# One layer of attention and routed experts on one core: gate/up and down products of a step set half a step apart

## The chip, the core and the metric

The kernel runs on one core of a Trainium2 chip. The metric is device time in microseconds (us), from launch to end. In the rows of the profile PE is TensorE, PEld its weight loads, DVE VectorE, ACT ScalarE, POOL GpSimd, and SPq the queue of SyncE, which issues most DMAs. Each engine takes its instructions in a fixed order that was written when the program was built; an instruction that waits for a semaphore holds up everything behind it on its engine.

## What is computed

Input x has 2048 tokens of 512 values, all in float32. The layer normalizes each token (xn), and adds three things to x:

```
rvk = xn @ W_rvk.T ; r, v, k = split(rvk)          # three products of 512 x 512 per token
y   = sigmoid(r) * wkv(time_decay, time_first, k, v)  # a recurrence along the tokens
attention = y @ W_out.T
logits = xn @ classifier.T ; two of 12 experts per token by softmax + bias
expert e < 8:  down_e( silu(gate_e(xn)) * up_e(xn) ),  inner width 256
expert e >= 8: xn itself                               # no weights
out = x + attention + sum of the two experts, each with its weight
```

## The kernel before

**Blocks and units.** The tokens are cut into four blocks of 512 (`b`) and each block into four rows of 128 tokens (`j`; row `i = 4b + j`, so 16 rows). The 512 channels are cut into four chunks (`c`). A unit is one (b, c): `project` (L259) makes k, v and r of it by three groups of four products, each 128x128 by 128x512, added up in a PSUM bank of the pool `ps_mm` (two banks). After the fourth product of a group ScalarE copies the bank to SBUF (L278 for k and v, L276 for r, an exponential); a new group waits for the copy of the group two before it. `scan` (L282) then runs the recurrence of the unit in four stages: VectorE prepares (L293 to L300); ScalarE takes two exponentials (L302, L303); VectorE makes the sums (L309 to L318); last come small copies of the state (POOL L321, ScalarE L322) and on VectorE a reciprocal (L323) and a product (L324). After the four chunks of a block, `attention` (L719) multiplies the block by W_out: four products for each row of 128 tokens, then VectorE adds the result to the row (L740), and an accumulating DMA on POOL's queue adds it to the output in DRAM (L743).

**Experts.** Routing is worked out early. Tokens are sorted by expert into 25 tiles of 128 places, and a tile goes through this chain, `i` being the tile:

- `gather` (POOL, L556): an indirect DMA fetches its 128 tokens.
- `flip` (ScalarE copy `xp`, L594; then a transposing DMA on SP, L596) and `unite` (ScalarE copy `xgT`, L602) turn the tokens so that they can be weights of a product.
- `fetch` (L574) and `fetch_down` (L579) load the expert's weights by SP's queue.
- `up` (L614, result `pg`): four products, gate and up side by side.
- `activate`: tanh on ScalarE (L622), two operations on VectorE (L623, L625).
- `flip_act` (ScalarE copy `ap`, L639; transposing DMA, L641) and `unite_act` (ScalarE copy `actT`, L646) turn the result.
- `finish`: two products with the down weights (L655, result `po`), a scaled copy on ScalarE (`yo`, L659), and an indirect DMA on POOL's queue that adds the rows to the output (L660).

All products are float32; each shows as two matmul records of the profile, so a group of four is "x8" in the rows, and a `finish` is "x4".

**Order.** From the fifth unit on the order of work is written by hand: a table of (time, work), sorted by time, from which instructions are issued one after the other on their engines. Units start every 19 table units, with stages at 0, 4, 6 and 12. The 36 groups of `project` and eight attention rows (blocks 0 and 1) are 44 groups spread evenly over the table (280.9 units); each group is issued whole. The 25 steps `step(i)` are set 10.68 units apart. A step does, in this order: fetch of i+2, `unite_act` of i-2, `flip_act` of i-1, `up` of i, `activate` of i, `gather` of i+3, `finish` of i-2, `flip` of i+2, `fetch_down` of i+1, `unite` of i+1. So in a step the down products of tile i-2 come right behind the gate/up products of tile i, and the `project` or attention groups lie between one step and the next.

Row i of attention reads its normalized tokens back from DRAM into `xrow` (`read_xn`, L706, pool `base` of four buffers), takes a PSUM bank of `ps_o` or `ps_mm`, and is added 3 table units after its products.

**The end.** Behind the table come the rows of block 2 (rows 8 to 11). Their `xrow` buffers are those of rows 4 to 7: the read of row 11 can't start before row 7's accumulating DMA has landed. Then a branch on the number of tiles (L812), not taken here, and block 3: the output rows so far are read back (L714), the row and the product are added on VectorE (L715, L737) and stored (L738). The read at L714 waits until POOL has passed its branch, and POOL passes it after it has issued the accumulating DMA of row 11. An expert's add to the output (L660) waits until all earlier adds have landed; a row add (L743) waits for the last expert add before it.

Of the kernel before, what the change touches and what calls it, by code (L numbers as in the profile page):

```python
# [26 lines left out]
F32 = mybir.dt.float32  # L27
# [8 lines left out]
P = 128  # L36
T = 2048
C = 512
CC = C // P
TB = 512  # L40
NTB = T // TB
NJ = TB // P
# [9 lines left out]
TILES = 25  # L52
# [7 lines left out]
def layer(ctx: ExitStack, tc: tile.TileContext, x, w_rvk, w_out, decay, first, cls, ebias, gu, down, out):  # L60
    nc = tc.nc

    def pool(name, bufs, **kw):
        return ctx.enter_context(tc.tile_pool(name=name, bufs=bufs, **kw))
# [18 lines left out]
    ps_tr = pool("ps_tr", 2, space=bass.MemoryType.PSUM)  # L83
# [412 lines left out]
    for m in range(2):  # L496
# [21 lines left out]
        for j in range(NT):  # L518
            k = m * NT + j
# [33 lines left out]
    def gather(i, token=token_i):  # L553

        xg = gathered.tile([P, C], F32, tag="xg", name=f"xg{i}")
        nc.gpsimd.indirect_dma_start(  # L556
            out=xg,
            out_offset=None,
            in_=xs,
            in_offset=bass.IndirectOffsetOnAxis(ap=token[:, i : i + 1], axis=0),  # L560
        )
        st[i] = {"xg": xg}

    def fetch(i, which=which_i):

        e = nc.values_load(
            which[0:1, i : i + 1],
            engines=(SP,),
            min_val=0,
            max_val=E - 1,  # L570
            skip_runtime_bounds_check_because="a sum of E - 1 comparisons",
        )
        w = ewp.tile([P, CC, 2 * INTER], F32, tag="gw", name=f"gw{i}")
        nc.sync.dma_start(w, gu[bass.ds(e, 1)].rearrange("o p c n -> p (o c) n"))  # L574
        st[i].update(w=w, e=e)

    def fetch_down(i):
        d = ewp.tile([P, IC, C], F32, tag="dw", name=f"dw{i}")
        nc.sync.dma_start(d, down[bass.ds(st[i]["e"], 1)].rearrange("o p c n -> p (o c) n"))  # L579
        st[i]["d"] = d  # L580
# [10 lines left out]
    def flip(i):  # L591

        xp = wk1.tile([P, 2, C], U16, tag="xp", name=f"xp{i}")
        nc.scalar.copy(xp, st[i]["xg"].bitcast(U16).rearrange("p (c h) -> p h c", h=2))  # L594
        xq = ex_p.tile([P, 2 * CC, P], U16, tag="xq", name=f"xq{i}")
        nc.sync.dma_start_transpose(xq, xp.rearrange("p h c -> p (h c)"))  # L596
        st[i]["xq"] = xq
# [10 lines left out]
    def up(i, cs):  # L608

        if 0 in cs:  # L610
            st[i]["pg"] = ps_gu.tile([P, 2, INTER], F32, tag="gu", name=f"pg{i}")
        pg = st[i]["pg"]
        for c in cs:
            nc.tensor.matmul(  # L614
                pg, st[i]["xgT"][:, c, :], st[i]["w"][:, c, :], start=(c == 0), stop=(c == CC - 1)
            )

    def activate(i):
        pg = st[i]["pg"]

        th = ex_p.tile([P, INTER], F32, tag="th", name=f"th{i}")
        nc.scalar.activation(th, pg[:, 0, :], AF.Tanh, scale=0.5)  # L622
        nc.vector.scalar_tensor_tensor(th, th, 1.0, pg[:, 0, :], ALU.add, ALU.mult)  # L623
        act = ex_p.tile([P, INTER], F32, tag="act", name=f"act{i}")
        nc.vector.tensor_mul(act, th, pg[:, 1, :])  # L625
        st[i]["act"] = act

    def turn_act(i):
        pt = ps_tr.tile([P, IC, P], F32, tag="tr", name=f"pa{i}")
        for c in range(IC):  # L630
            nc.tensor.transpose(pt[:, c, :], st[i]["act"][:, c * P : (c + 1) * P], ident)
        actT = ex_p.tile([P, IC, P], F32, tag="actT", name=f"actT{i}")
        nc.scalar.copy(actT, pt)
        st[i]["actT"] = actT

    def flip_act(i):

        ap = wk1.tile([P, 2, INTER], U16, tag="ap", name=f"ap{i}")
        nc.scalar.copy(ap, st[i]["act"].bitcast(U16).rearrange("p (c h) -> p h c", h=2))  # L639
        aq = wk1.tile([P, 2 * IC, P], U16, tag="aq", name=f"aq{i}")  # L640
        nc.sync.dma_start_transpose(aq, ap.rearrange("p h c -> p (h c)"))  # L641
        st[i]["aq"] = aq

    def unite_act(i):
        actT = ex_p.tile([P, IC, P], F32, tag="actT", name=f"actT{i}")
        nc.scalar.copy(  # L646
            actT.bitcast(U16).rearrange("p c (t h) -> p c t h", h=2),
            st[i]["aq"].rearrange("p (h c) t -> p c t h", h=2),
        )
        st[i]["actT"] = actT  # L650

    def finish(i, weight=wplace, to=to_i):
        po = ps_o.tile([P, C], F32, tag="o", name=f"po{i}")
        for c in range(IC):
            nc.tensor.matmul(  # L655
                po, st[i]["actT"][:, c, :], st[i]["d"][:, c, :], start=(c == 0), stop=(c == IC - 1)
            )
        yo = rows.tile([P, C], F32, tag="rb", name=f"yo{i}")
        nc.scalar.activation(yo, po, AF.Identity, scale=weight[:, i : i + 1])  # L659
        nc.gpsimd.indirect_dma_start(  # L660
            out=out,
            out_offset=bass.IndirectOffsetOnAxis(ap=to[:, i : i + 1], axis=0),
            in_=yo,
            in_offset=None,
            compute_op=ALU.add,
        )
        del st[i]

    def step(i, n):

        if i + 2 < n:
            fetch(i + 2)
        if i > 1:
            unite_act(i - 2)
        if 0 < i < n - 1:
            flip_act(i - 1)
        up(i, (0, 1))
        if i == n - 1:
            turn_act(i - 1)
        up(i, (2, 3))  # L680
        activate(i)
        if i + 3 < n:
            gather(i + 3)
        if i > 1:
            finish(i - 2)
        if i == n - 1:
            finish(i - 1)
        if i + 2 < n:
            flip(i + 2)
        if 2 <= i + 1 < n:  # L690
            fetch_down(i + 1)
        if i + 1 < n:
            unite(i + 1)

    xrows, orows = {}, {}
# [23 lines left out]
    def attention(b, js=range(NJ)):  # L719

        for j in js:
            i = b * NJ + j
            if j >= 2 if i in orows else b == NTB - 2 and j % 2 == 1:
                po = ps_mm.tile([P, C], F32, tag="mm", name=f"pw{i}")
            else:
                po = ps_o.tile([P, C], F32, tag="o", name=f"pw{i}")
            for c in range(CC):
                nc.tensor.matmul(  # L728
                    po,
                    yT[b][:, c, j * P : (j + 1) * P],  # L730
                    wout_sb[:, c, :],
                    start=(c == 0),
                    stop=(c == CC - 1),
                )
            yield
            if i in orows:
                nc.vector.tensor_add(orows[i], orows[i], po)  # L737
                nc.sync.dma_start(out[i * P : (i + 1) * P, :], orows[i])  # L738
            else:
                nc.vector.scalar_tensor_tensor(  # L740
                    xrows[i], xrows[i], zw[:, i : i + 1], po, ALU.mult, ALU.add
                )
                nc.gpsimd.dma_start(out[i * P : (i + 1) * P, :], xrows[i], accum_op=ALU.add)  # L743
            yield


    gather(0)
# [5 lines left out]
    stages = [scan(*u) for u in units]  # L753
# [15 lines left out]

    UNIT = 19.0  # L770
    ahead = [p for p in [project(*u) for u in units[LEAD:]] for _ in range(3)]
    after = {14: (0, 0), 17: (0, 1), 20: (0, 2), 23: (0, 3), 34: (1, 0), 37: (1, 1), 40: (1, 2), 43: (1, 3)}
    groups = len(ahead) + len(after)
    total = groups * 3.43 + TILES * 5.2
    table = []
    for u in range(1, len(units)):
        for k, at in enumerate((0, 4, 6, 12)):
            table.append(((u - 1) * UNIT + at, 1, stages[u]))
    for m in range(groups):
        at = total * m / groups  # L780
        if m in after:
            b, j = after[m]
            table.append((at - 16, 1, iter([(read_xn, b, [j])])))
            row = attention(b, [j])
            table += [(at, 1, row), (at + 3, 1, row)]
        else:
            table.append((at, CC, ahead.pop(0)))


    spread = (total - 14) / TILES  # L790
    for i in range(TILES):
        table.append((6 + spread * i, 1, iter([(step, i, TILES)])))
    table.append((6 + spread * TILES, 1, iter([(turn_act, TILES - 1)])))
    table.append((9 + spread * TILES, 1, iter([(finish, TILES - 1)])))
    for _, n, work in sorted(table, key=lambda entry: entry[0]):
        for _ in range(n):
            todo = next(work, None)
            if todo:
                todo[0](*todo[1:])
    read_xn(NTB - 2)  # L800
    read_xn(NTB - 1)
    whole(attention(NTB - 2))
    manual.close()

# [24 lines left out]

    read_out(NTB - 1)  # L830
    whole(attention(NTB - 1))


# [40 lines left out]
```

## Time and profile before

| | us |
|---|---|
| median of 9 runs (lowest, highest) | 397.0 (394.88, 398.48) |
| the profiled execution's own time | 397.08 |
| its span, first to last instruction | 395.3 |
| TensorE busy | 375.6 (95%) |
| VectorE busy | 271.0 (69%) |
| ScalarE busy | 170.6 (43%) |
| POOL busy | 98.6 (25%) |

The span is divided as follows: TensorE starts at 9.66 us, the routing and the first four units last until 81 us, the table with its 25 tiles until about 361 us, and the rest is the end described above. In a row of the timeline the columns are the start, the duration, the engine, the line, the operation, the tiles written and read, the number of instructions merged, and in brackets the idle time ahead of it with what ended it. A matmul's duration covers its passage through the pipeline; the distance of two starts tells more. Four products of a group start 3.43 us before the next group.

### The profile page before, as it was taken

The page shows a single profiled execution, that of the slowest core. Times are in us where ns is not written, and L with a number is a line of the kernel's source. Part 1 is how long each engine was busy: PE and PEld are TensorE (multiplying, and loading weights), DVE is VectorE, ACT ScalarE, POOL GpSimd, SP SyncE. Part 2 cuts the span into 40 slices and gives each one's busy share as a digit, 9 for nine tenths or more (in the row PEclk, how much of TensorE's full clock was granted, in tenths as well). Part 3 has the DMA queues.
Part 4 walks back from the last instruction along what each step waited for, and adds up shares of the span by engine and source line. Part 5 has one row for each costly group of instructions (what it writes and reads, how often), then busy time and mean ns, then how long its engine had stood idle before and what let it go on. Part 6 is the DMA issues. An engine that isn't in the chain of part 4 may idle for free. (4 is left out here: it accounts for less than half of the span.)

```text
span 395.3 us, 3511 instructions
## 1 busy us (share of the span) xinstructions
PE 375.6 (95%) x994; PEld 169.7 (43%) x994; DVE 271.0 (69%) x397; ACT 170.6 (43%) x278; POOL 98.6 (25%) x130
## 2 busy tenths in 40 slices
PE   0999999999999999999999989999999999999995
PEld 0545444444444434444444434444444444443431
DVE  5872998997857557769576583976857658858305
ACT  2765111553564455636353644655553455322000
POOL 4002001321040342312224232422330312133300
PEclk9999999999999999999999999999999999999999
DMA  7998908455689868979998989799999899742794
GB/s 264 407 388 330 319 28 326 116 170 168 205 240 248 251 170 219 211 229 276 263 245 189 292 141 309 191 277 244 259 265 266 234 198 241 192 75 33 95 253 158
DMA packets 62885, 88.80 MB, mean 225 GB/s; under 512 B 42192, under 2 KB 42320, under 8 KB 59088
## 3 DMA queue, kind: packets, MB, share of 16 engines
q1 hardware_dynamic: 55328, 67.85, 56.8%
q0 software_dynamic: 7536, 20.71, 26.4%
q8 instruction: 8, 0.13, 0.1%
q14 instruction: 13, 0.11, 0.1%
HBM read 63.78 MB, written 19.40 MB: 210 GB/s over the span
## 5 line engine op out<-in xcount | busy, mean ns | idle before, releaser
L614 PE MATMUL pg<-gw,xgT 128*128 128x512 f32 x200 | 90.2, 593 | 1.2 <-ACT xgT L602 1.2
L660 POOL DMA_INDIRECT out_dram<-yo,to_i x25 | 42.7, 1707 | 135.9 <-ACT yo L659 80.6
L265 PE MATMUL pk<-xnT,wrvk 128*128 128x512 f32 x128 | 58.8, 596 | 0.0
L614 PEld LDWEIGHTS pg<-gw,xgT 128*128 128x128 f32 x200 | 37.8, 190 | 48.9 <-issue 45.0
L728 PE MATMUL pw<-wout_sb,yT 128*128 128x512 f32 x128 | 57.0, 594 | 1.4 <-ACT yo L659 0.8
L265 PE MATMUL pr<-xnT,wrvk 128*128 128x512 f32 x128 | 57.7, 592 | 0.0
L265 PE MATMUL pv<-xnT,wrvk 128*128 128x512 f32 x128 | 57.6, 593 | 0.0
L323 DVE RECIPROCAL den<-den 128x512 f32<-128x512 f32 x16 | 53.5, 3344 | 0.0
L309 DVE TENSOR_TENSOR_SCAN sums<-obv,state,a 128x512 f32<-128x512 f32 x16 | 20.5, 1282 | 40.2 <-ACT obv L303 40.2
L655 PE MATMUL po<-dw,actT 128*128 128x512 f32 x100 | 46.9, 593 | 1.0 <-ACT actT L646 1.0
L556 POOL DMA_INDIRECT xg<-xs,token_i x25 | 30.5, 1219 | 43.3 <-DVE empty L543 27.4
L623 DVE SCALAR_TENSOR_TENSOR th<-th,pg 128x256 f32<-128x256 f32 x25 | 10.5, 419 | 42.6 <-ACT th L622 42.6
L728 PEld LDWEIGHTS pw<-wout_sb,yT 128*128 128x128 f32 x128 | 24.0, 190 | 32.6 <-issue 29.7
L265 PEld LDWEIGHTS pk<-xnT,wrvk 128*128 128x128 f32 x128 | 23.8, 190 | 31.9 <-issue 31.4
L265 PEld LDWEIGHTS pr<-xnT,wrvk 128*128 128x128 f32 x128 | 24.2, 190 | 30.1 <-issue 30.1
L265 PEld LDWEIGHTS pv<-xnT,wrvk 128*128 128x128 f32 x128 | 24.2, 190 | 30.1 <-issue 29.9
L659 ACT ACTIVATE yo<-po,wplace 128x512 f32<-128x512 f32 x25 | 17.2, 687 | 35.1 <-PE po L655 35.1
L655 PEld LDWEIGHTS po<-dw,actT 128*128 128x128 f32 x100 | 18.9, 190 | 25.2 <-issue 22.6
L594 ACT COPY xp<-xg 128x1024 uint16<-128x1024 uint16 x25 | 25.9, 1037 | 8.5 <-DMA xg<-xs,token_i 5.2
L602 ACT COPY xgT<-xq 128x1024 uint16<-128x1024 uint16 x25 | 29.0, 1160 | 0.0
L622 ACT ACTIVATE th<-pg 128x256 f32<-128x256 f32 x25 | 9.6, 384 | 44.4 <-PE pg L614 44.3
L743 POOL DMA_DIRECT2D out_dram<-xrow x12 | 11.1, 1008 | 57.4 <-DMA out_dram<-yo,to_i 38.2
(151 smaller groups left out, 368.8 us busy)
## 6 DMA issues: line engine op xcount, KB each, us to landing
gw<-in_gu_dram SPq DMA_DIRECT2D x25, 1024.0 KB, 7.2
dw<-in_down_dram SPq DMA_DIRECT2D x25, 512.0 KB, 5.5
x<-in_x_dram SPq DMA_DIRECT2D x16, 256.0 KB, 5.4
xs<-x SPq DMA_DIRECT2D x16, 256.0 KB, 5.2
wrvk<-in_w_rvk_dram SPq DMA_DIRECT2D x3, 1024.0 KB, 7.5
xrow<-xs SPq DMA_DIRECT2D x12, 256.0 KB, 5.5
out_dram<-xrow POOLq DMA_DIRECT2D x12, 256.0 KB, 5.4
wout_sb<-in_w_out_dram SPq DMA_DIRECT2D x1, 1024.0 KB, 10.2
```

Source lines behind the costliest of these rows:

```text
L265: nc.tensor.matmul(ps, wrvk_sb[m][:, k, c * P : (c + 1) * P], xnT[b][:, k, :], start=(k == 0), stop=(k == CC - 1),)
L309: nc.vector.tensor_tensor_scan(sq, bs, a2, s[:, 3:4], ALU.add, ALU.mult)
L323: nc.vector.reciprocal(den, den)
L556: nc.gpsimd.indirect_dma_start(out=xg, out_offset=None, in_=xs, in_offset=bass.IndirectOffsetOnAxis(ap=token[:, i : i + 1], axis=0),)
L594: nc.scalar.copy(xp, st[i]["xg"].bitcast(U16).rearrange("p (c h) -> p h c", h=2))
L602: nc.scalar.copy(xgT.bitcast(U16).rearrange("p c (t h) -> p c t h", h=2), st[i]["xq"].rearrange("p (h c) t -> p c t h", h=2),)
L614: nc.tensor.matmul(pg, st[i]["xgT"][:, c, :], st[i]["w"][:, c, :], start=(c == 0), stop=(c == CC - 1))
L655: nc.tensor.matmul(po, st[i]["actT"][:, c, :], st[i]["d"][:, c, :], start=(c == 0), stop=(c == IC - 1))
L659: nc.scalar.activation(yo, po, AF.Identity, scale=weight[:, i : i + 1])
L660: nc.gpsimd.indirect_dma_start(out=out, out_offset=bass.IndirectOffsetOnAxis(ap=to[:, i : i + 1], axis=0), in_=yo, in_offset=None, compute ...
L728: nc.tensor.matmul(po, yT[b][:, c, j * P : (j + 1) * P], wout_sb[:, c, :], start=(c == 0), stop=(c == CC - 1),)
L743: nc.gpsimd.dma_start(out[i * P : (i + 1) * P, :], xrows[i], accum_op=ALU.add)
```

## The change

`step` is split. `first_half(i)` holds fetch, `flip_act`, `up`, `activate` and `gather`; `second_half(i)` holds `unite_act` and `finish` of tile i-2, then `flip`, `fetch_down` and `unite` as before. The second half stands 5.34 table units behind the first, and `unite_act` of i-2 has moved from the head of the step, ahead of `up`, to directly ahead of its `finish`. Groups are no longer issued whole: each of their four products has its own place in the table, 1.6 units apart, so that a half step can fall between two products of one group. Attention rows of blocks 0 and 1 stand in pairs (groups 14 and 15, 20 and 21, 34 and 35, 42 and 43), both rows of a pair are added after the second, and rows 0 to 5 take their bank from the pool `ps_tr`. The number of instructions of each kind is unchanged. Some lines have other numbers in the changed kernel: L706 is L708, L714 is L716, L715 is L717, L728 is L732, L737 is L741, L740 is L744, L743 is L747 and L812 is L822; up to L665 they are the same.

```diff
-    def step(i, n):
+    def first_half(i, n):
         if i + 2 < n:
             fetch(i + 2)
-        if i > 1:
-            unite_act(i - 2)
         if 0 < i < n - 1:
             flip_act(i - 1)
         up(i, (0, 1))
...
         activate(i)
         if i + 3 < n:
             gather(i + 3)
+
+    def second_half(i, n):
+
         if i > 1:
+            unite_act(i - 2)
             finish(i - 2)
...
-            if j >= 2 if i in orows else b == NTB - 2 and j % 2 == 1:
+            if i < (NTB - 2) * NJ - 2:
+                po = ps_tr.tile([P, C], F32, tag="tr", name=f"pw{i}")
+            elif j >= 2 if i in orows else j % 2 == 1:
                 po = ps_mm.tile([P, C], F32, tag="mm", name=f"pw{i}")
...
-            yield
+                yield
...
-    after = {14: (0, 0), 17: (0, 1), 20: (0, 2), 23: (0, 3), 34: (1, 0), 37: (1, 1), 40: (1, 2), 43: (1, 3)}
+    after = {14: (0, 0), 15: (0, 1), 20: (0, 2), 21: (0, 3), 34: (1, 0), 35: (1, 1), 42: (1, 2), 43: (1, 3)}
...
+    one = total / groups / CC
     for m in range(groups):
-        at = total * m / groups
         if m in after:
             b, j = after[m]
-            table.append((at - 16, 1, iter([(read_xn, b, [j])])))
-            row = attention(b, [j])
-            table += [(at, 1, row), (at + 3, 1, row)]
+            group = attention(b, [j])
+            plan(CC * m * one - 16, read_xn, b, [j])
+
+            plan(CC * (m + 2 - j % 2) * one + 1, group)
         else:
-            table.append((at, CC, ahead.pop(0)))
+            group = ahead.pop(0)
+        for k in range(CC):
+            plan((CC * m + k) * one, group)
...
     for i in range(TILES):
-        table.append((6 + spread * i, 1, iter([(step, i, TILES)])))
+        plan(6 + spread * i, first_half, i, TILES)
+        plan(6 + spread * (i + 0.5), second_half, i, TILES)
```

## Prediction

> **What bounds the kernel.** I read the page first, then the waits, then the timeline around every wait of TensorE. The page's first part: TensorE is busy nearly always, and no other engine is near it.
>
> ```profile
> PE 375.6 (95%) x994; PEld 169.7 (43%) x994; DVE 271.0 (69%) x397; ACT 170.6 (43%) x278; POOL 98.6 (25%) x130
> ```
>
> Of the 19.7 us in which it isn't busy, 9.66 lie ahead of the first product and 4.7 behind the last (390.6 to 395.3). The waits of TensorE name the rest:
>
> ```profile
> PE pg L614 <- ACT xgT L602: 1.2, 1, 1.2
> PE po L655 <- ACT actT L646: 1.0, 1, 1.0
> ```
>
> So in the table (81 to 361 us) only these two, 2.16 us together, can be won: TensorE takes a product each 3.43 / 4 = 0.858 us, in a fixed order, and the change adds or removes none. What counts is whether ScalarE delivers in time for the new order. Its turnaround is in the timeline (start, duration, engine, line):
>
> ```profile
> 139.60 3.60 PE L265 MATMUL pv<-xnT,wrvk 128*128 128x512 f32 x8
> 139.80 0.69 ACT L659 ACTIVATE yo<-po,wplace 128x512 f32<-128x512 f32 x1 [1.33 <-PE po L655]
> 140.39 1.03 ACT L594 COPY xp<-xg 128x1024 uint16<-128x1024 uint16 x1
> 141.32 1.16 ACT L602 COPY xgT<-xq 128x1024 uint16<-128x1024 uint16 x1
> ...
> 146.88 0.67 ACT L646 COPY actT<-aq 128x512 uint16<-128x512 uint16 x1
> ...
> 147.60 1.98 PE L655 MATMUL po<-dw,actT 128*128 128x512 f32 x4 [0.98 <-ACT actT L646]
> ...
> 156.49 0.59 ACT L278 COPY k<-pk 128x512 f32<-128x512 f32 x1 [2.84 <-PE pk L265]
> 156.97 0.63 ACT L302 ACTIVATE a<-a 128x512 f32<-128x512 f32 x1
> ```
>
> The first row is the product that follows a `finish`, so `po` ended at 139.60; ScalarE begins `yo` 0.20 later, `xp` 0.59 after that, `xgT` 0.93 after that. A wait on `actT` ends 0.72 after `actT` starts (146.88 to 147.60), and the first product after a wait takes 0.10 more (1.98 against 1.88). A group's copy also starts 0.20 after its products, and the next operation 0.48 after it (156.49 to 156.97). For `xgT` the other wait gives 1.20 from its start to the product:
>
> ```profile
> 233.68 1.15 ACT L602 COPY xgT<-xq 128x1024 uint16<-128x1024 uint16 x1
> ...
> 234.89 3.70 PE L614 MATMUL pg<-gw,xgT 128*128 128x512 f32 x8 [1.18 <-ACT xgT L602]
> ```
>
> Hence two turnarounds. From the end of a `po` to the next `pg`: 0.20 + 0.59 + 0.93 + 1.20 = 2.92. From the end of a group to a `po` whose `actT` stands behind the group's copy: 0.20 + 0.48 + 0.72 = 1.40. Before, four products of `up` (3.43) lie between `unite_act` and its `po`, and at least one whole group (3.43) between `po` and the next `pg`; that is why only two of 50 waits show.
>
> **The change, step by step.** I counted the products in the changed kernel's built order on TensorE, and what stands ahead on ScalarE.
>
> *a. `po` to the next `pg`.* Between them now stand 3 products (2.57) ahead of tiles 3, 4, 6, 7, 9, 10, 13, 14, 16, 17, 19, 20, 22 and 23, and 4 (3.43) ahead of the other eight. With 3 the wait is 2.92 + 0.10 - 2.57 = 0.45; with 4 nothing. 14 x 0.45 = 6.3 us. Tile 1's `pg` has three products behind a copy, `xp` and `xgT`: 0.48 + 0.93 + 1.20 + 0.20 + 0.10 - 2.57 = 0.3.
>
> *b. `pg` to the `po` half a step later.* `unite_act` has lost the cover of `up` and stands on ScalarE behind the copy of any group that ends in the 3 or 4 products between. Where a group ends directly ahead of the `po` (tiles 1, 4, 7, 13, 16, 19, 22) the wait is the whole 1.40 + 0.10 = 1.5: 7 x 1.5 = 10.5. Where it ends one product earlier (tiles 0, 3, 9, 12, 15, 21): 1.50 - 0.86 = 0.64, 6 x 0.64 = 3.8. Two products earlier or more, or where the group is an attention row that ScalarE doesn't copy: nothing (tiles 2, 5, 6, 10, 11, 14, 18, 20). State copies (L322) ahead of the copy add 0.1 twice: 0.2.
>
> *c. Exponentials ahead of `unite_act`.* For tiles 8 and 17 ScalarE has L302 and L303 between, and VectorE makes their input only after `activate` of the same first half. The rows of that chain:
>
> ```profile
> 95.17 0.38 ACT L622 ACTIVATE th<-pg 128x256 f32<-128x256 f32 x1 [2.33 <-PE pg L614]
> 95.58 0.42 DVE L623 SCALAR_TENSOR_TENSOR th<-th,pg 128x256 f32<-128x256 f32 x1 [2.15 <-ACT th L622]
> 96.04 0.42 DVE L625 TENSOR_TENSOR act<-th,pg 128x256 f32<-128x256 f32 x1
> ...
> 96.45 1.27 DVE L297 TENSOR_TENSOR_SCAN obv<-wdec,state,k 128x512 f32<-128x512 f32 x1
> 97.76 0.75 DVE L299 SCALAR_TENSOR_TENSOR a<-obv,wdec 128x512 f32<-128x512 f32 x1
> 98.43 0.69 DVE L300 TENSOR_TENSOR obv<-k,obv 128x512 f32<-128x512 f32 x1
> ```
>
> `pg` ended 0.20 ahead of the first; L300 ends at 99.12, 4.15 after `pg`. The second exponential then takes 0.54 to the next start, and `actT` 0.72: 5.4, with 0.10: 5.5. Tile 8 has 3 products between (5.5 - 2.57 = 2.9), tile 17 four (5.5 - 3.43 = 2.1): 5.0 us. Elsewhere the exponentials stand a step behind their inputs.
>
> *d. What goes.* The 1.18 came from a gather late on POOL behind a row add; `gather` now has a step and a half ahead of its `xp` instead of one. The 0.98 came from a state copy ahead of `unite_act`. With the 0.10 each: -2.4. What is late next is a to c.
>
> *e. Moved at no cost.* `aq` has half a step more. `fetch`, `fetch_down`, `flip` and `unite` keep one to three steps to their use, in the same order on SP; the row reads between them wait for adds that landed long before. Row pairs put two adds on POOL ahead of an expert's add, which only delays the expert's add (`yo` has three buffers). If the gather's cover went, a wait like the 1.18 would be back. The `ps_tr` banks have no other use until tile 23's `turn_act`.
>
> *f. The end.* The last stretch is no matter of TensorE but of adds in series:
>
> ```profile
> 364.01 1.54 POOL L660 DMA_INDIRECT out_dram<-yo,to_i  x1 [4.14 <-issue]
> 369.43 2.70 POOL L743 DMA_DIRECT2D out_dram<-xrow  x3 [3.87 <-DMA out_dram<-yo,to_i]
> ...
> 379.88 0.86 POOL L743 DMA_DIRECT2D out_dram<-xrow  x1 [5.68 <-DVEq L812]
> ...
> 382.37 1.82 SPq L714 DMA_DIRECT2D orows<-out_dram  x4
> ```
>
> Tile 24's add, then row 7's at 369.43; when that has landed SP reads row 11 (373.54), VectorE adds it (378.84), TensorE goes on with the product that needs its bank (379.64), POOL issues it, and the output is read back (382.37). In the new order row 6's add is no longer early: it stands behind tile 24's and ahead of row 7's, which so lands second. In the trace row 7's landing is followed by row 8's 2.2 later (373.5, 375.7). Bounds: nothing, if both land together; 4.1, if row 7's waits for all of row 6's (369.43 to 373.5). I take 2.2, the row that shows two in line. The three products won ahead of tile 24's `po` bring nothing, since its add waits for tile 23's.
>
> **The sum.** 6.3 + 0.3 + 10.5 + 3.8 + 0.2 + 5.0 = 26.1; less 2.4; and 2.2 at the end: +25.9 us. 397.08 + 25.9 = 423.0 us. The profiled execution is 0.08 from the median, so the same holds for that.
>
> **A rule on the clock.** The rows: after 9.66 idle us the first eight `lg` products (L239) took 2.64 us, later ones 1.07; after the waits of 0.98 and 1.18 products went on each 0.43, granted clock 1.000. [...]
>
> **Rivals.**
> *Faster (the other side).* ScalarE is busy only 43%, and the half steps give each of its results a stretch of other products; if the turnaround were fully covered, only d would be left: 397.08 - 2.4 = 394.7 without the tail's cost, 396.9 with it. It decides at 1.40 us between a group's end and its `po` and 2.92 from `po` to `pg`. Against it: seven tiles have no product there at all.
> *Half the loss.* TensorE fetches weights ahead and ends are modelled, so waits under 0.7 might vanish; then 10.5 + 5.0 + 0.2 - 2.4 + 2.2 = +15.5: 412.6.
> *More.* The exponentials of five more tiles (1, 3, 10, 12, 19) stand ahead of a `unite_act`; if VectorE, 69% busy and with a reciprocal of 3.34 in its queue, were late there as in c, 2 to 3 us each: +10 to +15, 433 to 438. Behind the `pg` of the step before it VectorE has 0.6 + 0.9 (tanh, L623, L625), 4.0 (L323, L324) and 2.6 (L293 to L300) = 8.1 us of work, and 2.57 + 1.72 + 3.43 + 3.43 = 11.1 us to do it, so I don't take it.
> *The change doesn't do what it says.* The built order shows that it does (TensorE's list has 301 stretches, was 263).
>
> **Chances.** Forecast, +20 to +33: 0.70. Half the loss, +2 to +20: 0.15. More: 0.09. Faster: 0.04, no change 0.02. The range, 411 to 432, leaves out "more", no change, faster and the lower part of half the loss; its ends are a to c without the short waits and without the tail's 2.2 (410.4), and the sum with the tail's 4.1 and two or three of the five tiles late. A difference under 0.3% (1.2 us) can't be told from no change: faster 0.04, same 0.02, slower 0.94.
>
> **What would show it.** In the waits of TensorE of the changed kernel: `po` L655 waiting for `actT` L646 some 15 times, 19 us, longest 2.9; `pg` L614 for `xgT` L602 some 15 times, 5 to 6 us; TensorE's busy time as before, so a share near 89%. Row 11's read should start 2.2 us later behind tile 24's add than now. I am wrong if those waits are few and short, or if another releaser (VectorE, a gather, a weight load by SP) ends them.

## The result, and the profile after

The changed kernel takes 423.73 us (median of 10 runs, 422.09 to 426.44) beside 396.63 us for the kernel before: a ratio of 1.0681, 95% interval 1.0655 to 1.0707. The forecast was 423.0 us. (A median is of all runs of a kernel; a ratio goes by the fast runs, those within 1.5% of a kernel's quickest.) The profiled execution took 422.69 us, with a span of 420.9 us. First its page, the line of busy times:

```profile
PE 384.2 (91%) x994; PEld 168.1 (40%) x994; DVE 270.8 (64%) x397; ACT 169.8 (40%) x278; POOL 93.3 (22%) x130
```

The same 994 matmul records; VectorE and ScalarE do the same work in the same time and POOL in less. No engine has become the bound; the span is longer because TensorE waits. Who ends its waits stands in the waits view of the same kernel (columns: total us, times, longest):

```profile
PE po L655 <- ACT actT L646: 15.9, 15, 2.8
...
PE pg L614 <- ACT xgT L602: 2.8, 14, 0.2
PE pw L732 <- DVE xrow L744: 2.1, 1, 2.1
```

Left out is the start of the kernel, as before. The two waits of before, 1.2 on `xgT` and 1.0 on `actT`, are gone, and in their place stand 15 waits on `actT` and 14 on `xgT`, all ended by a ScalarE copy. The third wait, for a row at the end, was there before with 0.52 us (its rows follow below). Waits of both kinds, in the timeline of TensorE:

```profile
107.28 1.98 PE L655 MATMUL po<-dw,actT 128*128 128x512 f32 x4 [0.48 <-ACT actT L646]
109.10 2.74 PE L265 MATMUL pr<-xnT,wrvk 128*128 128x512 f32 x6
112.04 3.70 PE L614 MATMUL pg<-gw,xgT 128*128 128x512 f32 x8 [0.20 <-ACT xgT L602]
115.58 3.60 PE L265 MATMUL pk<-xnT,wrvk 128*128 128x512 f32 x8
...
120.43 1.98 PE L655 MATMUL po<-dw,actT 128*128 128x512 f32 x4 [1.25 <-ACT actT L646]
...
205.07 1.98 PE L655 MATMUL po<-dw,actT 128*128 128x512 f32 x4 [2.75 <-ACT actT L646]
```

Read these by starts. Tile 0's `po` and the three `pr` products start at 107.28 and 109.10; three products are 2.57 us, so `pg` could have started at 111.68 and starts at 112.04: 0.37 lost, of which the row shows 0.20 as idle, and 0.10 more in the slower first product. Tile 1's `po` stands directly behind a whole group: 115.58 + 3.43 = 119.01, it starts at 120.43. Tile 8 is the one with the exponentials ahead of `actT`. The rest of a wait (0.16 to 0.17 us, and the 0.10) is booked as busy: the profile models the ends of matmuls, and a row of four products shows 3.60 us where the starts are 3.43 apart. That, 29 times, and a stretch at half clock near the end (1.55 us, see f below) are why PE busy rose by 8.6 us with the same products.

From the first `pg` to tile 22's `po`, with the same number of products between (TensorE's list), the kernel before took 348.51 - 81.23 = 267.28 us, the changed one 372.64 - 81.38 = 291.26: 23.98 more. From there to the end it was 46.79 and is 48.26: 1.47 more. The rows of tile 22's `po` and of the last products, first of the kernel before, then of the changed one:

```profile
348.51 3.60 PE L655 MATMUL po<-dw,actT 128*128 128x512 f32 x8
...
379.64 10.96 PE L728 MATMUL pw<-wout_sb,yT 128*128 128x512 f32 x24 [0.52 <-DVE xrow L740]
```

```profile
372.64 3.70 PE L655 MATMUL po<-dw,actT 128*128 128x512 f32 x8 [1.25 <-ACT actT L646]
...
404.37 12.51 PE L732 MATMUL pw<-wout_sb,yT 128*128 128x512 f32 x24 [2.05 <-DVE xrow L744]
```

### The profile page after: what moved, and what is told of

Its sections match the earlier page's. It is cut to its first block, busy times and chain, and to the rows that moved or that the text cites. A ratio compares the mean times of both kernels' runs of the same rounds, so it can differ in the third digit from the quotient of the medians.

```text
span 420.9 us, 3515 instructions
## 1 busy us (share of the span) xinstructions
PE 384.2 (91%) x994; PEld 168.1 (40%) x994; DVE 270.8 (64%) x397; ACT 169.8 (40%) x278; POOL 93.3 (22%) x130
## 5 line engine op out<-in xcount | busy, mean ns | idle before, releaser
L614 PE MATMUL pg<-gw,xgT 128*128 128x512 f32 x200 | 91.6, 600 | 2.9 <-ACT xgT L602 2.8
L655 PE MATMUL po<-dw,actT 128*128 128x512 f32 x100 | 48.4, 608 | 15.9 <-ACT actT L646 15.9
L732 PE MATMUL pw<-wout_sb,yT 128*128 128x512 f32 x128 | 58.9, 607 | 2.2 <-DVE xrow L744 2.1
L265 PE MATMUL pk<-xnT,wrvk 128*128 128x512 f32 x128 | 60.3, 596 | 0.0
L265 PE MATMUL pv<-xnT,wrvk 128*128 128x512 f32 x128 | 59.4, 593 | 0.0
L265 PE MATMUL pr<-xnT,wrvk 128*128 128x512 f32 x128 | 59.4, 592 | 0.0
L614 PEld LDWEIGHTS pg<-gw,xgT 128*128 128x128 f32 x200 | 36.7, 190 | 55.5 <-issue 38.3
L732 PEld LDWEIGHTS pw<-wout_sb,yT 128*128 128x128 f32 x128 | 24.7, 195 | 33.9 <-issue 30.8
L655 PEld LDWEIGHTS po<-dw,actT 128*128 128x128 f32 x100 | 17.7, 189 | 45.1 <-ACT actT L646 29.5
L556 POOL DMA_INDIRECT xg<-xs,token_i x25 | 25.5, 1022 | 44.6 <-DVE empty L543 27.5
L230 PE MATMUL pt<-ident,x 128*128 128x128 f32 x64 | 12.3, 324 | 11.2 <-DVE x L220 9.8
```

Of the source, the lines that this page charges most:

```text
L230: nc.tensor.transpose(pt[:, j * P : (j + 1) * P], xt[b * NJ + j][:, c * P : (c + 1) * P], ident)
L265: nc.tensor.matmul(ps, wrvk_sb[m][:, k, c * P : (c + 1) * P], xnT[b][:, k, :], start=(k == 0), stop=(k == CC - 1),)
L556: nc.gpsimd.indirect_dma_start(out=xg, out_offset=None, in_=xs, in_offset=bass.IndirectOffsetOnAxis(ap=token[:, i : i + 1], axis=0),)
L614: nc.tensor.matmul(pg, st[i]["xgT"][:, c, :], st[i]["w"][:, c, :], start=(c == 0), stop=(c == CC - 1))
L655: nc.tensor.matmul(po, st[i]["actT"][:, c, :], st[i]["d"][:, c, :], start=(c == 0), stop=(c == IC - 1))
L732: nc.tensor.matmul(po, yT[b][:, c, j * P : (j + 1) * P], wout_sb[:, c, :], start=(c == 0), stop=(c == CC - 1),)
```

## The experiments

The theory was that of the forecast: ScalarE's turnaround, uncovered twice in each step. Its rivals were that breaking the groups into single products costs by itself, that the half step costs by itself, and that the clock of TensorE makes up a good part. All kernels stood beside runs of the kernel before on the same chip (medians 396.5 to 397.5 there); ratios go by these.

**`unite_act` early.** `unite_act` goes back to the head of the step, half a step ahead of its `po`; all else stays as changed.

```diff
 def first_half(i, n):
+    if i > 1:
+        unite_act(i - 2)
...
 def second_half(i, n):
     if i > 1:
-        unite_act(i - 2)
         finish(i - 2)
```

> The changed kernel, but unite_act of tile i-2 is back at the head of the first half, ahead of up, so that its copy actT has four more products (3.43 us) of cover. Theory (ScalarE's turnaround): the waits of po (L655) for actT, b and c of the sum, 19.5 us, go; those of pg (L614) for xgT stay; 423.7 - 19.5 = 404.2 us. Rival (splitting groups into single products costs time by itself, by changing weights and banks between products): little changes, the waits move to another releaser, over 415 us. Rival (short idle lowers the clock): besides the 19.5 the lost clock comes back, about 402 us and a granted clock nearer 1.

Measured: 401.88 us, ratio 1.0129 (1.0080 to 1.0177). The waits view:

```profile
PE pg L614 <- ACT xgT L602: 2.7, 14, 0.2
```

All 15 waits on `actT` are gone, the 14 on `xgT` are untouched. 21.8 us came back. Steps b and c make 19.5 of them, and from the first `pg` to tile 22's `po` the profile has 271.44 us, 19.82 less than the changed kernel's. The other 2 us are what the rival of the clock named (402 us, a clock nearer 1): the mean clock is 0.9985 in the median of these four runs, 0.992 in the changed kernel's; but the four runs spread from 399.64 to 403.42. The rival of the single products falls: they are all still there.

**`unite` early.** The mirror image: the copy `xgT` of the next tile is issued ahead of `finish` instead of behind it.

```diff
 def second_half(i, n):
     if i > 1:
         unite_act(i - 2)
+    if i + 1 < n:
+        unite(i + 1)
+    if i > 1:
         finish(i - 2)
...
-    if i + 1 < n:
-        unite(i + 1)
```

> The changed kernel, but unite of tile i+1 (the copy xgT) stands ahead of finish in the second half, so that it no longer waits for po, yo and xp. Theory (turnaround): the waits of pg for xgT, a of the sum, go, 6.6 us with tile 1's; those of po for actT stay as they are; 423.7 - 6.6 = 417.1 us. Rival (the 0.20 us that the waits view shows for each of them is all there is, 14 x 0.20): only 2.8 us, 420.9. Rival (single products cost by themselves): no change.

Measured: 417.03 us, ratio 1.0532 (1.0493 to 1.0571). Now the other family is gone:

```profile
PE po L655 <- ACT actT L646: 15.9, 15, 2.8
```

6.7 us came back where step a and tile 1 have 6.6. This kernel's profile also shows 6.8 us of half clock (granted clock 0.50) directly behind tile 8's wait, which the changed kernel's profile does not have at that wait; more on that below. In the changed kernel's half-clock stretch (405.28 to 408.69) the weight loads, one to a record, start 0.85 us apart, and 0.43 behind it. At that rate a stretch of 3.4 us does half its work, which costs some 1.7 us, an estimate. From the first `pg` to tile 22's `po` this profile has 287.48 us; without the 3.4 lost there that is 7.2 less than the changed kernel's 291.26, so the agreement of the medians to 0.1 is partly luck.

**Both early.** The two edits together.

> The changed kernel with both moves: unite_act at the head of the first half, unite ahead of finish; half step, single products and paired rows stay. Theory (turnaround): a, b and c go, 26.1 us: 397.6 us, no wait of TensorE between 81 us and the end. Rival (half step, single products or pairs cost something besides): over 403 us.

Measured: 394.71 us, ratio 0.9955 (0.9927 to 0.9984). Half step, single products and pairs are all in it, and it is 0.5% quicker than the kernel before. It is 2.9 us below what was expected: from the first `pg` to tile 22's `po` 26.31 us are gone (forecast 26.1), and most of the clock that the changed kernel loses, which the expectation had kept, is back (mean clock 0.9985 in the median of the runs, 0.992 in the changed kernel). Between the first `pg` and the end only one wait is left:

```profile
PE pw L733 <- DVE xrow L745: 1.5, 1, 1.5
```

**Without the half step.** `unite_act` early, and the second half directly behind the first; single products and pairs stay.

```diff
-    plan(6 + spread * (i + 0.5), second_half, i, TILES)
+    plan(6 + spread * i, second_half, i, TILES)
```

> The changed kernel without its half step: the second half directly behind the first, unite_act at the head as in the kernel before; single products and paired rows stay. po then follows pg as before, and 6 or 7 products lie between po and the next pg (5.1 to 6.0 us against 2.92 needed). Theory (turnaround): no waits, 397.6 us, as with both copies early. Rival (single products or pairs cost by themselves): over 403 us. If this one is fast and the one with both copies early is not, the half step has a second cost that I have not named.

Measured: 393.78 us, ratio 0.9939 (0.9905 to 0.9973), 3.8 below what was expected. Its profile has one wait of 1.1 us, for the copy of `r` (L276), and none in the tail: here tile 22's `po` stands 3 products earlier, 2.57 us, and with it the adds that the tail waits for.

**The half step alone.** The kernel before with `step` split as in the change, `unite_act` in the second half, but whole groups and rows apart.

> The kernel before with the half step alone: groups of four products stay whole and rows stay apart. ScalarE's turnaround has then either a whole group or nothing to hide behind. By the turnaround: 15 tiles have a whole group directly ahead of po, 13 x 1.5 and two with exponentials 2.1 each = 23.7; three po directly behind pg, 0.20 + 0.36 + 0.72 + 0.10 = 1.4 each = 4.2; two such with exponentials ahead, 2.4 to 5.5 each; three pg directly behind po, 3.0 each = 9.0; less 2.4 won: 396.5 + 39 to 46 = 436 to 442 us, and up to a few us of half-speed stretches on top. Rival, the loss comes from breaking the groups into single products and the half step alone costs nothing: 395 to 398.

Measured: 447.95 us (442.87 to 451.37) beside 397.34 of the kernel before. By the two quickest of its four runs, 442.87 and 446.10, the half step without single products costs 46 to 49 us, the whole change 27. Its waits:

```profile
PE po L655 <- ACT actT L646: 29.3, 20, 2.3
...
PE pg L614 <- ACT xgT L602: 8.3, 3, 2.8
```

The turnaround gave 436 to 442. The profiled execution (span 444.3) has five half-speed stretches, 5 x 1.7 = 8.5 us, on top. So the single products don't cost: with them a half step falls between the products of a group, the waits on `actT` are 13.4 us less (15.9 against 29.3) and those on `xgT` 5.5 us less (2.8 against 8.3), some two fifths of what the half step costs.

**Single products alone.** No half step and `unite_act` at the head, as in the version without the half step, and rows apart as in the kernel before.

```diff
-    after = {14: (0, 0), 15: (0, 1), 20: (0, 2), 21: (0, 3), 34: (1, 0), 35: (1, 1), 42: (1, 2), 43: (1, 3)}
+    after = {14: (0, 0), 17: (0, 1), 20: (0, 2), 23: (0, 3), 34: (1, 0), 37: (1, 1), 40: (1, 2), 43: (1, 3)}
...
-            plan(CC * (m + 2 - j % 2) * one + 1, group)
+            plan(CC * (m + 1) * one + 1, group)
```

> Single products alone: no half step, rows apart as in the kernel before. If single products by themselves remove the two waits of before (1.18 and 0.98 us with 0.10 each), as the version with pairs and without the half step did (393.8): 394.0. Rival, it is the pairing of the rows that takes the row adds out of the way of the gathers on POOL: the 1.18 us stays, 395.5 to 396.5.

Measured: 401.31 us (396.41 to 405.62), ratio 1.0064 (1.0020 to 1.0108), 2.5 us by the ratio: neither. The body is as quick as with pairs (first `pg` to tile 22's `po` 263.78 us, with pairs 263.39, the same products between). The loss is in the tail, in POOL's timeline:

```profile
353.00 1.54 POOL L660 DMA_INDIRECT out_dram<-yo,to_i  x1 [3.74 <-ACT obv L303]
358.25 0.92 POOL L748 DMA_DIRECT2D out_dram<-xrow  x1 [3.70 <-DMA out_dram<-yo,to_i]
362.88 1.60 POOL L660 DMA_INDIRECT out_dram<-yo,to_i  x1 [3.71 <-issue]
```

Row 6's add now falls between those of tiles 23 and 24, and each waits for the last to land: tile 24's add is 9.88 us behind tile 23's, where the version with pairs has 5.88 (353.03 to 358.91). What the pairs do is to move row 6 out of that place. (The third stage of the last unit also stands at 8 instead of 6 table units here, which was not tried by itself.)

**`yo` four times.** The changed kernel with one suspected cost made larger.

```diff
+        for _ in range(4):
-        nc.scalar.activation(yo, po, AF.Identity, scale=weight[:, i : i + 1])
+            nc.scalar.activation(yo, po, AF.Identity, scale=weight[:, i : i + 1])
```

> The changed kernel with ScalarE's yo issued four times instead of once, 3 x 0.59 = 1.77 us more between a po and the next xgT; output unchanged. If ScalarE's turnaround is what pg waits for: 14 tiles wait 0.45 + 1.77 = 2.2 us and the eight with four products between them 2.92 + 1.77 + 0.10 - 3.43 = 1.4, so 14 x 1.77 + 8 x 1.36 = 35.7 us more: 459 us, waits of pg on xgT 35 to 40 us in 22 places. On the clock: if waits of 1.4 to 2.2 us lower it each time, 22 x 1.7 = 37 us more on top (about 495, mean clock near 0.92); if only now and then, 460 to 467. Rival, the waits for xgT are set by its transposed read or by the gather and not by ScalarE's queue: 424 to 430.

Measured: 479.00 us (476.20 to 482.83), ratio 1.2086 (1.2016 to 1.2157). The waits, and a group on ScalarE:

```profile
PE pg L614 <- ACT xgT L602: 43.1, 22, 2.4
PE po L655 <- ACT actT L646: 15.9, 15, 2.7
```

```profile
123.93 2.85 ACT L660 ACTIVATE yo<-po,wplace 128x512 f32<-128x512 f32 x4 [2.08 <-PE po L655]
126.67 1.03 ACT L594 COPY xp<-xg 128x1024 uint16<-128x1024 uint16 x1
```

22 places, as counted from the order; the 15 others don't move. Four `yo` take 126.67 - 123.93 = 2.74 to the next start, so 2.15 more than one and not 1.77, and the waits grew by 40.3 where 35.7 were expected. The profile has seven half-speed stretches of 3.4 us, the changed kernel's one: about 10 us more. 420.9 + 40.3 + 10 = 471, measured span 474.4; of the rest 1.6 us are waits for a `yo` near the end. So the theory of the turnaround holds where its cost is quadrupled, and the clock comes now and then, not at each wait.

**The tail: row 6 early.** Both copies early, and row 6 (group 40) added ahead of tile 22's add, as in the kernel before.

```diff
-    after = {..., 42: (1, 2), 43: (1, 3)}
+    after = {..., 40: (1, 2), 43: (1, 3)}
...
-            plan(CC * (m + 2 - j % 2) * one + 1, group)
+            plan((CC * (m + 2 - j % 2) if m < 40 else CC * (m + 1)) * one + 1, group)
```

(With it, the third stage of the last unit moves from 6 to 8 table units, as for single products alone.)

> Both ScalarE copies early (394.7 us), and row 6's product and add moved to before tile 24's add, as in the kernel before. If the tail's cost is the late row 6 and the half-speed stretch of TensorE that follows the wait for row 11: the wait of pw on xrow falls from 1.5 us to about 0.5 and the clock stays full to the end, so 1.0 + 1.7 us less in executions with that stretch: 392.5. Rival, the end is held by the adds of tiles 22 to 24 whatever row 6 does: 394.7, with the wait still there.

Measured: 396.22 us beside 397.34, ratio 0.9958 (0.9921 to 0.9994); with row 6 late it was 0.9955. The time is the rival's. Counted from the first `pg` (82.06 with row 6 late, 80.58 early), tile 22's add goes out at 267.83 with row 6 late and at 268.87 with it early, since row 6's add now stands directly ahead of it; row 7's add goes out at 284.59 and 285.14. It still lands earlier with row 6 early, at 289.08 against 290.31, as step f has it. But the read of row 11 behind it took 6.99 us in this profile, 4.72 with row 6 late, and TensorE waits 2.9 us for row 11 instead of 1.5. Why the read took longer is not shown. So step f named a part of the path that is there, but most of it is taken back: by row 6's add ahead of tile 22's, and here by the read.

**The tail: rows 8 to 11 in a buffer of their own.** They are read into a `gw` buffer, as those of block 3 are, free after tile 22's gate/up products; so the read of row 11 no longer waits for row 7's add. Done to the changed kernel, to the version with both copies early, and to that without the half step.

```diff
-        if b == NTB - 1:
+        if b >= NTB - 2:
             t = ewp.tile([P, NJ, C], F32, tag="gw", name=f"xrows{b}")
...
-            if b == NTB - 1:
+            if b >= NTB - 2:
                 xrows[i] = t[:, j, :]
```

> The changed kernel, with rows 8 to 11 read into one buffer that is free after tile 22's gate/up products, so that the read of row 11 no longer waits for the add of row 7 to land. If the tail's cost is that wait of TensorE (2.05 us) and the half-speed stretch behind it (1.7 us when it comes): no wait of pw on xrow, full clock from tile 17 to the end, 423.7 - 2.05 = 421.7, or down to 420.0 where the stretch went too. Rival, the end is held by the row adds and the read of the output behind them: 423.7.

Measured: 420.74 us, ratio 1.0589 (1.0547 to 1.0632), where the changed kernel has 1.0681. The wait on `xrow` is gone, and the median lies between the two figures expected: 2.05 for the wait and part of a half-speed stretch. In the profile the stretch from tile 22's `po` to the end is 44.38 us, 3.88 less.

> The same rows edit in the version with both ScalarE copies early (0.9955 of the kernel before). No wait of TensorE is left between the first gate/up product and the end, so the 1.5 us and the half-speed stretch behind it go: 391.5 to 393 us beside a kernel before at 397. Rival, adds and read-back hold the end: 0.9955 again.

Measured: 391.83 us (391.16 to 392.46), ratio 0.9868 (0.9834 to 0.9903): as expected, and the fastest of all. From its page:

```profile
PE 373.7 (96%) x994; PEld 169.7 (44%) x994; DVE 271.1 (70%) x397; ACT 170.6 (44%) x278; POOL 94.1 (24%) x130
```

TensorE waits for nothing from the first `pg` to its last product; the runs lie within 1.3 us.

> The same rows edit in the version without the half step (0.9939). Its profile shows no wait in the tail, but its runs spread from 391.4 to 397.9; if a late row 11 makes the slower ones, the spread closes and the median falls to 392.5; if not, 393.8 as before. A 1.1-us wait for a k/v/r copy stays in it.

Measured: 393.67 us (391.98 to 398.10), ratio 0.9895 (0.9854 to 0.9936); the time and the spread stay, so row 11 was not what spread the runs. This profile, of a run of 397.53 us, shows its one wait of over 0.2 us behind the first `pg`, and what ScalarE stood at:

```profile
PE pv L265 <- ACT r L276: 3.6, 1, 3.6
```

```profile
241.04 1.04 ACT L594 COPY xp<-xg 128x1024 uint16<-128x1024 uint16 x1 [4.34 <-DMA xg<-xs,token_i]
...
244.10 0.57 ACT L276 ACTIVATE r<-pr 128x512 f32<-128x512 f32 x1
```

ScalarE waits 4.34 us for a gather that POOL issued at 231.25, behind a pair of row adds issued at 229.06, and the copy of `r` stands behind it. It was 1.85 in the profile without the rows edit. With the half step the gather has half a step more. In the two profiles with the half step and both copies early TensorE has no such wait; ScalarE waits 2.69 us for a gather in the one without the rows edit and for none in the one with it. That this is what the half step is good for is likely but not shown: these are single profiles, and the intervals of 0.9868 and 0.9895 overlap.

## Why the prediction was right

**a. `po` to `pg`: right.** 14 places with three products between, as counted, and nothing with four. Forecast 6.3; by the waits view 2.8 idle + 14 x (0.17 + 0.10) = 6.6. Undoing it alone gave 6.7.

**b and c. `pg` to `po`: right.** 15 waits, in the tiles named: 1.42 and 0.10 at tile 1, 0.64 and 0.10 at tile 0 (104.06 + 2.57 = 106.64 to 107.28), 2.92 at tile 8 and 2.06 at tile 17 (311.21 to 313.27). Forecast 19.5 in all; 15.9 + 15 x (0.16 + 0.10) = 19.8. No tile of the rival "more" waits for exponentials. "Half the loss" fails by the short waits: they cost 0.37 and 0.64 between starts although the page books less than that as idle. For the same reason TensorE's share was 91%, not the 89% I named: I had taken a wait to be idle time in full.

**d and e. What goes, and what costs nothing: right.** With both copies early the body takes 347.01 - 82.06 = 264.95 us for the same products, 2.3 less than before (forecast 2.4). The body as a whole: +23.98, forecast 23.7.

**f. The end: sum near, its parts wrong.** Forecast 2.2 for row 7's add landing second, measured 1.47. The delay is there: row 7 lands 2.1 behind row 6 (398.73 and 396.61), and the read of row 11 starts 11.47 us behind tile 24's add (387.31 to 398.78), before 9.53: 1.94 later. But the adds before came quicker: tiles 22 to 24 go out at 375.63, 381.33 and 387.31, 5.70 and 5.98 apart, before 6.20 and 6.37; and the read of row 11 took 4.58 us, before 5.17. Against the start of tile 22's `po` row 11 is ready only 0.6 later than before. TensorE, which gets there earlier, waits 2.05 us instead of 0.52, and behind that wait comes a half-speed stretch: the last 24 records of the kernel's products took 12.51 us instead of 10.96, 1.55 more. About 0.7 is given back at the very end, where the chain now ends on TensorE's products and no longer on the adds: 0.6 + 1.55 - 0.7 = 1.45. Without the clock, then, the term was about 0 and not 2.2. Moving row 6 back brought nothing; taking away row 11's dependence on row 7 did.

**The clock: a sum without a term for it failed.** The sum went by the two waits seen before, 0.98 and 1.18 us, behind which the clock stayed at 1.000. The runs show half-speed stretches behind waits of 1.9 to 3.6 us (2.05 in the changed kernel, 2.75 in the one with rows 8 to 11 in their own buffer), and one behind a wait of 1.49 (both copies early). Their size is in the mean clock of the runs: 0.986 to 0.996 in the changed kernel (0.992 in the median), 0.993 to 1.000 (0.999) in the kernel before. One stretch of 3.4 us is 0.004 of the span and costs some 1.7 us, by the estimate above. From the median before, the body and the end without the clock give 396.63 + 23.98 - 0.08 = 420.5 us; the 3.2 that are left are what one and a half to two such stretches cost, as the mean clock has it. So a to d met by their mechanism, but the sum met the time to 0.7 us by luck: two terms were off and cancelled, the end by 2.3 too much, the clock by 3.2 too little.

## What to carry to other kernels

When a step is split or moved to shorten one wait, count for every product on the bound engine what now stands between its producer's start and itself: ScalarE, busy only 40%, still needed its 1.4 or 2.9 us of turnaround each time, and it was the order in its queue, not its load, that covered them. Issue the copy a product needs as early as its input allows, ahead of work that waits for the same engine; the split then costs nothing here (0.9955 with it, 0.9939 without). Where adds to one output run in series, look for a buffer that is tied to one of them.

## What the runs showed of the hardware

In these profiles the clock of TensorE fell by a grid in time, not by the length of a wait. In every one the half-speed stretches ahead of the program's last microseconds last 3.41 us or a multiple of it (405.28 to 408.69 in the changed kernel), and start whole numbers of 3.41 us apart (there the next one, behind the last product, starts at 418.93: 13.65 later, 4 x 3.41). The windows view, cut along that grid, for the changed kernel (columns: stretch, length, busy time of each engine with the instructions, granted clock, DMA share and rate). First the tail's wait, then tile 8's:

```profile
401.87:405.28 3.41, 1.36 (x4) 0.30 (x2) 1.41 (x2) 0.00 (x0) 1.33 (x2) 1.00 0.85 317
405.28:408.69 3.41, 3.26 (x5) 1.46 (x5) 0.00 (x0) 0.00 (x0) 0.41 (x1) 0.50 1.02 125
...
200.48:203.89 3.41, 1.84 (x5) 0.53 (x3) 3.18 (x6) 1.28 (x3) 0.62 (x1) 1.00 0.81 253
203.89:207.31 3.42, 2.24 (x5) 1.06 (x6) 2.79 (x3) 1.35 (x3) 0.00 (x0) 1.00 1.01 236
```

The wait of 2.05 us lies in one window, of which products cover 1.36 us, 0.40 of it: the next window runs at 0.50. The wait of 2.75 us straddles a border, both windows are covered for over half, and nothing happens. In the changed kernel with rows 8 to 11 in their own buffer the same wait of 2.75 us falls otherwise on the grid:

```profile
201.80:205.21 3.41, 0.81 (x2) 0.00 (x0) 2.62 (x4) 1.72 (x3) 0.00 (x0) 1.00 1.00 272
205.21:208.62 3.41, 3.26 (x4) 1.51 (x5) 3.37 (x4) 0.10 (x1) 0.00 (x0) 0.50 0.47 114
```

Over 13 profiles (the kernel before, the changed one and the eleven above), between 60 us and 14 us ahead of the end, some 1,280 such windows at full clock or half: all 17 that were covered for 0.42 or less were followed by half speed; of those at 0.43 to 0.46 two were and three weren't; above, only one at 0.52 was, in the tail of the version with both copies early, and why it was stays open. Once a half-speed window itself was followed by another, when products had covered 0.81 of it (the 6.8 us of "`unite` early"). So two executions of one program can differ by some 1.7 us, an estimate from the 3.41 us at half speed, for each wait of the length of these, 2.05 and 2.75 us, by where it falls.

Products over up to 0.42 of a window weren't enough to keep the full clock. Short idle did nothing by itself: the 27 waits of 0.2 to 1.4 us in the changed kernel's profile are followed by no half-speed stretch.
